# Build order of the adjacency tiles in a graph network kernel: halves of the four densest tiles placed between the others

## Chip, cores and metric

The kernel runs on one core of one Trainium2 chip. The metric is the device time of one execution in microseconds (us); below, the median of three executions and one execution with the hardware profiler.

## What is computed

The graph has 6250 nodes with 64 features and 200000 edges, sorted by destination. Destinations follow 6250 u² with u uniform, so low node numbers have many more edges than high ones. Two layers of mean aggregation (SAGE) come first, then three message-passing layers, each block with a residual and a layer norm:

```python
def sage_conv(x, src, dst, W_l, b_l, W_r, n_nodes):
    agg = segment_sum(x[src], dst, n_nodes)
    cnt = segment_sum(ones, dst, n_nodes)
    return agg / maximum(cnt, 1.0) @ W_l.T + b_l + x @ W_r.T

h = relu(sage_conv(x, ..., W_l1, b_l1, W_r1)); out = sage_conv(h, ..., W_l2, b_l2, W_r2)
x = layernorm(x + out)

def _mp_layer(x, src, dst, ea, W, b):      # self loops added
    m = concatenate([x[dst], x[src], ea], axis=1) @ W.T + b
    return relu(segment_sum(m, dst, n))
# three such layers, batch norm and relu after the first two
x = layernorm(x + _mp_layer(...))
```

Every aggregation is the same product: the matrix A of edge counts (source by destination) times node features. The kernel builds A once and uses it five times.

## The kernel before

**A in tiles.** Nodes are padded to NB = 49 blocks of 128. A is cut by destination into NT = 13 tiles of 512 columns (the last has 128, with 106 nodes). A tile `a` is [128, 49 x 512] in fp8: row p of block h is source 128 h + p. Its buffers come from the pool `fadj` with three buffers, which also holds, at the start, the edge list and the search table (`scratch`, L729).

**Windows and slots.** `window_plan` (L434) divides each tile's destinations into windows of w neighbouring nodes and gives each window k slots, a slot being 128 edges, from the expected number of edges alone. The plan has 2569 slots. By tile, 0 to 12: 655, 280, 256, 190, 171, 171, 171, 149, 128, 128, 128, 120 and 22. Dense tiles have narrow windows (one node at first, several slots each), later tiles wide ones (four nodes, one slot each). The windows of tile 0 average 92 columns (49 w) a slot, those of tile 8 have 196. Slots are numbered in build order and grouped by 128 into the columns t of a table. Where the edges of a window start is found by a search on the device (`near_samples`, `first_edges`, L787 to L820), in five groups of table columns; `SEARCH` (L417) says at which t each group's two steps are issued. `columns(t)` (L859) gathers the edges of 128 slots with one indirect DMA on GpSimd's queue and makes the keys: source low part, and source high part combined with the destination in the window.

**Build of a tile** (`build`, L896). For each slot, DVE makes two one-hot matrices by comparison with an iota (`one_hots`, L598): `lo` (128 columns, for 16 slots at a time, three buffers) and `rhs` (49 w columns, for a run of slots, three buffers). PE multiplies them into `pair` (L931), a PSUM tile of two banks, two buffers. When both banks are complete, ACT writes them to the fp8 tile (L938 for two equal banks at once, L943 one by one). After its last window the tile is stored to DRAM on SP's queue (L947). The last tile is first cleared by a memset on GpSimd (L903).

**First layer** (`first_layer`, L684). As soon as a tile is built, it is used from SBUF: `aggregate` (L618) issues 4 x 49 matmuls of 193 columns (L628: three bf16 parts of the features and a column of ones for the count) into one PSUM tile `agg` from a pool with one buffer. DVE reads it (L689, L653), counts are inverted (L690, L691, L695), and PE and ACT go on with a transpose (L678), a product (L698), a relu, a product (L703) and the split of the result into the bf16 parts of the second layer's input (L705 to L709).

**Order.** The loop at L1003 emits tile j's build and then the first layer of tile j - 1. A scheduler with its own cost model then fixes the order on each engine, so that matmuls of aggregation and build alternate on PE. [...] After the loop the slot buffers and PSUM banks are released (`slots.close()`), and the first layer of the last two tiles follows. `relative_dst` (L965), three DVE operations, and 72 small index loads on SP's queue (L959) prepare the edge attributes; they are emitted during the build.

**Second layer and the rest.** The second layer (L1032) starts with tiles 0 and 1 together, reloaded from DRAM (`load_adj`, L655): with `src_first` it goes over the 49 source blocks b and for each over the eight destination blocks, so that it can begin before the last blocks of the second layer's input exist. Beside it the edge attributes are summed (L976, L997). The three message layers (L1128) use A again.

Of the kernel before, what the change touches and what calls it, by code (L numbers as in the profile page):

```python
# [15 lines left out]
I32 = mybir.dt.int32  # L16
# [6 lines left out]
P = 128  # L23
TW = 512
# [427 lines left out]
    return tiles  # L452


@with_exitstack
def gnn_kernel(ctx: ExitStack, tc: tile.TileContext, x, src, dst, ea, W_l1, b_l1, W_r1, W_l2, b_l2, W_r2,
               W0, b0, W1, b1, W2, b2, g0, be0, g1, be1, out):
# [21 lines left out]
    def tw(j):  # L479
        return min(TW, NPAD - j * TW)  # L480

    wins = window_plan(N, E)
    slot_of, table = [], []
    for ws in wins:
        for d0, w, k in ws:
            slot_of.append(len(table))
            table += [(d0, s * P) for s in range(k)]
    NS = len(table)
    R = -(-NS // P)
# [1 line left out]
    for b in range(NB):  # L491
        n, c = slots_for(expected(N, E, b * P, (b + 1) * P)), 0
# [34 lines left out]
    adj8 = [dram.tile([P, NB * tw(j)], mybir.dt.uint8, name=f"adj8_{j}") for j in range(NT)]  # L527
    ok_t = None

    with ExitStack() as fast:  # L530
# [12 lines left out]
        apool = fast.enter_context(tc.tile_pool(name="fadj", bufs=3))  # L543
# [71 lines left out]
            w = tw(j)  # L615
            return a[:, : NB * w].rearrange("p (i w) -> p i w", w=w).bitcast(F8)

        def aggregate(psa, pt, tiles, n, src_first=False, feed=None, terms=None):  # L618

            views = [view(a, j) for a, j in tiles]
            sums = [psa.tile([P, 4, TW // 2], F32, name="agg") for _ in tiles]
            blocks = [(k, i) for k, (_, j) in enumerate(tiles) for i in range(tw(j) // P)]

            def product(k, i, b):

                nc.tensor.matmul(sums[k][:, i, :n], views[k][:, b, i * P: (i + 1) * P], pt[:, b, :n],  # L628
                                 start=(b == 0 and terms is None and not (src_first and i % 2)), stop=(b == NB - 1),
                                 skip_group_check=src_first or terms is not None)  # L630

            def term(k, i):
                if terms is not None:
                    at = tiles[k][1] * TW + i * P
                    nc.tensor.matmul(sums[k][:, i, : terms[1].shape[1]], terms[0][:, at: at + P], terms[1],  # L635
                                     start=not (src_first and i % 2), stop=False, skip_group_check=True)

            if src_first:
                for k, i in blocks:
                    term(k, i)  # L640
                for b in range(NB):
                    feed(b)
# [69 lines left out]
        with ExitStack() as bld:  # L712
# [180 lines left out]
                    made[c // HOT] = lo  # L893
                return made[c // HOT][:, c % HOT, :]

            def build(j):  # L896

                a = apool.tile([P, NB * TW], mybir.dt.uint8, name="a")
                av = view(a, j)
                ws = wins[j]  # L900
                done = sum(len(q) for q in wins[:j])
                if (j + 1) * TW > N:
                    nc.gpsimd.memset(a.bitcast(I32), 0)  # L903

                todo, banks, at = [], [], 0
                for q, (d0, w, k) in enumerate(ws):
# [4 lines left out]
                    todo += [(slot_of[done + q] + s, w * NB, len(banks) - 1, at, s == 0, s == k - 1) for s in range(k)]  # L911
                    at += w * NB

                runs = []
# [6 lines left out]
                pair = rhs = None  # L921
                for e, (slot, wc, bank, col, first, last) in enumerate(todo):
# [18 lines left out]
                    else:  # L941
                        for two, (o, nd) in enumerate(of):
                            nc.scalar.activation(av[:, :, o: o + nd],  # L943
                                                 pair[:, two, : nd * NB].rearrange("p (d h) -> p h d", h=NB),
                                                 AF.Copy, saturate=False)
                eng = nc.sync
                eng.dma_start(adj8[j], a[:, : NB * tw(j)])  # L947
                return a

            ids = room[:, 2 * size: 2 * size + 4 * NSUB * EAG].bitcast(I32).rearrange("p (i g) -> p i g", g=EAG)  # L950
# [48 lines left out]
                    if i == last_b[b]:  # L999
                        nc.scalar.activation(ext[:, b * P: (b + 1) * P], ps[:, :P], AF.Identity, bias=selfl)  # L1000

            prev = None
            for j in range(NT):  # L1003
                a = build(j)
                if j == 7:
                    relative_dst()
                if j == NT - 1:
                    break
                if prev is not None:
                    first_layer(psa1, prev, j - 1)  # L1010
# [188 lines left out]
```

## Time and profile before

| | |
|---|---|
| median of three executions | 1677.59 us (1675.6 to 1678.23) |
| profiled execution | 1678.72 us |
| its span, first to last instruction | 1676.9 us |
| granted TensorE clock, mean | 0.962 |
| busy PE, DVE, ACT | 1499.6, 923.4, 580.8 us |
| first build matmul starts | 43.36 us |
| stores of the built tiles 0 to 12 start (L947) | 167.1, 222.8, 261.9, 306.9, 344.3, 378.1, 411.8, 447.8, 482.7, 516.9, 551.2, 594.6, 608.9 us |
| aggregation (L628), whole kernel | 12005 matmuls, 1103.1 us busy |
| build matmuls (L931) | 2569 matmuls, 264.5 us busy |
| one-hots for the build on DVE (L598), lo and rhs | 194.8 and 236.0 us busy |
| evictions on ACT (L938) | 292.3 us busy |

Busy time is the union of an engine's instructions. The line of an operation made in a helper is that of the helper, so the one-hots of the build and of the edge attributes share L598. A matmul's end is modelled, so the busy time of PE also contains some waiting. "Waited" times name the instruction that came last. In a row of the stage table, the mark (x...) counts instructions.

### The profile page before, as it was taken

The numbers are of one execution on the slowest core, as the hardware profiler recorded it, in microseconds if no ns is written. First come the engines' busy times: TensorE is split into PE (matmuls) and PEld (weight loads), VectorE is DVE, ScalarE is ACT, GpSimd is POOL, SyncE is SP. The second block draws the span as 40 slices with busy tenths as digits, with TensorE's granted clock in tenths as the row PEclk, the third lists the DMA queues.
The fourth block names the chain that finished last, engine by engine and source line by source line (L and its number), as shares of the span: only waits on it lengthen the run. The fifth ranks groups of instructions, "written<-read, shape, count | busy, mean of one in ns | idle before, by whom it ended". The sixth has DMA issues, their size and how long they took to land.

```text
span 1676.9 us, 38592 instructions
## 1 busy us (share of the span) xinstructions
PE 1499.6 (89%) x17135; PEld 1383.0 (82%) x17135; DVE 923.4 (55%) x1581; ACT 580.8 (35%) x1085; POOL 82.3 (5%) x72
## 2 busy tenths in 40 slices
PE   1454989999999889999999999999999999999997
PEld 0343877788888779889999989988899999899997
DVE  2999999998788741988787721011241110342122
ACT  1233466787688640454454400000220000210000
POOL 2223100000000110000000000000000000000000
PEclk9965999999999989999999999999899999899999
DMA  5111232113211153635452634343416352345440
GB/s 161 30 29 50 97 93 83 80 81 152 86 78 78 79 205 159 259 138 182 144 204 75 248 143 166 154 169 130 184 58 251 155 218 110 155 166 231 165 183 10
DMA packets 43811, 228.10 MB, mean 136 GB/s; under 512 B 22978, under 2 KB 30210, under 8 KB 35826
## 3 DMA queue, kind: packets, MB, share of 16 engines
q1 hardware_dynamic: 37058, 139.54, 22.1%
q10 hardware_dynamic: 4496, 79.48, 12.1%
q0 software_dynamic: 2080, 6.52, 1.4%
q8 instruction: 136, 2.23, 0.5%
q14 instruction: 41, 0.34, 0.1%
HBM read 183.76 MB, written 41.75 MB: 134 GB/s over the span
## 4 chain that ended last, share of the span: by engine, by line
PE 62%; DVE 21%; ACT 7%; issue 5%; DMA 3%; ACTq 0%; POOL 0%; DVEq 0%; POOLq 0%
PE agg L628 47%; DVE lo L598 8%; PE pair L931 6%; ACT a L938 4%; DVE rhs L598 4%; PE u L1079 2%; PE bank L997 2%; DMA a<-adj 1%; PE agg L635 1%; DVE e L990 1%; DVE e L988 1%; DVE nd L653 1%; PE lin L1100 1%; PE lin L698 1%; PE tr L678 1%
## 5 line engine op out<-in xcount | busy, mean ns | idle before, releaser
L628 PE MATMUL agg<-parts,a 128*128 128x192 bf16 (+1 forms) x12005 | 1103.1, 248 | 7.6 <-DVE nd L653 4.8
L628 PEld LDWEIGHTS <-a 128*128 128x128 fp8e3 x12005 | 1012.5, 98 | 32.6 <-issue 17.4
L938 ACT ACTIVATE a<-pair 128x784 fp8e3<-128x784 f32 (+3 forms) x357 | 292.3, 886 | 120.8 <-PE pair L931 119.1
L931 PE MATMUL pair<-rhs,lo 128*128 128x147 bf16 (+5 forms) x2569 | 264.5, 243 | 73.6 <-DVE lo L598 50.2
L931 PEld LDWEIGHTS <-lo 128*128 128x128 bf16 x2569 | 195.9, 105 | 121.1 <-DVE lo L598 66.1
L598 DVE TENSOR_TENSOR rhs<-iota,k 128x1960 bf16<-128x1960 f16 (+14 forms) x240 | 236.0, 1006 | 12.8 <-ACT k L883 7.0
L598 DVE TENSOR_TENSOR lo<-iota,k 128x2048 bf16<-128x2048 f16 x161 | 194.8, 1220 | 0.0
L653 DVE TENSOR_REDUCE z<-agg 128x256 f32<-128x768 f32 (+1 forms) x39 | 35.3, 910 | 282.7 <-PE agg L628 282.4
L598 DVE TENSOR_TENSOR lo<-iota,e_d 128x2048 bf16<-128x2048 f16 (+11 forms) x132 | 130.9, 1012 | 20.6 <-PE bank L997 19.9
L997 PE MATMUL bank<-lo,lhs 128*128 128x128 bf16 x1701 | 107.6, 220 | 16.2 <-ACT lhs L991 10.8
L997 PEld LDWEIGHTS <-lhs 128*128 128x128 bf16 x1701 | 98.4, 98 | 27.4 <-ACT lhs L991 18.2
L653 DVE TENSOR_REDUCE nd<-agg 128x256 f32<-128x768 f32 (+1 forms) x26 | 23.5, 907 | 116.0 <-PE agg L628 116.0
L680 ACT COPY mx<-tr 128x512 f32<-128x512 f32 (+1 forms) x26 | 14.6, 560 | 177.5 <-PE tr L678 177.5
L1087 DVE BATCH_NORM_STATS2 stats<-hr 64x6 f32<-64x512 f32 (+1 forms) x26 | 17.0, 652 | 101.7 <-ACT hr L1102 80.4
L669 ACT ACTIVATE sp_r<-z 128x256 f32<-128x256 f32 (+1 forms) x26 | 10.5, 403 | 171.5 <-DVE z L668 171.4
L1116 ACT ACTIVATE hr<-tr 64x512 f32<-64x512 f32 (+1 forms) x13 | 7.4, 566 | 179.9 <-PE tr L1115 179.9
L987 ACT CAST lhs<-e 128x512 bf16<-128x512 f32 (+21 forms) x72 | 36.1, 502 | 58.9 <-PE bank L997 44.6
L991 ACT CAST lhs<-e 128x512 bf16<-128x512 f32 (+21 forms) x72 | 36.4, 505 | 23.0 <-DVE e L990 22.4
L988 DVE TENSOR_TENSOR e<-e,lhs 128x512 f32<-128x512 f32 (+21 forms) x72 | 39.5, 552 | 8.3 <-ACT lhs L987 8.2
L989 ACT CAST lhs<-e 128x512 bf16<-128x512 f32 (+21 forms) x72 | 36.3, 504 | 22.2 <-DVE e L988 21.1
L990 DVE TENSOR_TENSOR e<-e,lhs 128x512 f32<-128x512 f32 (+21 forms) x72 | 39.4, 548 | 7.3 <-ACT lhs L989 6.7
L864 POOL DMA_INDIRECT rows<-cmb_d,start_i x21 | 30.8, 1465 | 251.0 <-ACT key L875 207.4
(140 smaller groups left out, 784.8 us busy)
## 6 DMA issues: line engine op xcount, KB each, us to landing
a<-adj SPq DMA_DIRECT2D x24, 3136.0 KB, 11.8
a<-adj ACTq DMA_DIRECT2D x24, 3136.0 KB, 11.3
adj<-a SPq DMA_DIRECT2D x12, 3136.0 KB, 9.8
e<-in_edge_attr_dram SPq DMA_DIRECT2D x25, 256.0 KB, 2.6
a<-adj SPq DMA_DIRECT2D x4, 784.0 KB, 4.6
out_dram<-z SPq DMA_DIRECT2D x12, 128.0 KB, 14.3
a<-first_edges ACTq DMA_DIRECT2D x1, 1216.0 KB
e<-in_edge_attr_dram SPq DMA_DIRECT2D x7, 152.0 KB
```

Source lines behind the costliest of these rows:

```text
L598: nc.vector.tensor_tensor(to.rearrange("p g (h two) -> p g h two", two=2), iota[:, :n].rearrange("p (h two) -> p h two", two=2).unsqueeze( ...
L628: nc.tensor.matmul(sums[k][:, i, :n], views[k][:, b, i * P: (i + 1) * P], pt[:, b, :n], start=(b == 0 and terms is None and not (src_first ...
L653: nc.vector.tensor_reduce(to, ps[:, :nb, : 3 * D].rearrange("p b (r d) -> p b d r", r=3), AX.X, ALU.add)
L931: nc.tensor.matmul(pair[:, bank % 2, col: col + wc], lo_hot(t, c), rhs[:, i, :wc], start=first, stop=last)
L938: nc.scalar.activation(av[:, :, o: o + 2 * nd].rearrange("p h (two d) -> p h two d", two=2), pair[:, :, : nd * NB].rearrange("p two (d h) ...
L987: nc.scalar.copy(lhs[:, :g, 0:EC], r)
L988: nc.vector.tensor_sub(r, r, lhs[:, :g, 0:EC])
L989: nc.scalar.copy(lhs[:, :g, EC:2 * EC], r)
L990: nc.vector.tensor_sub(r, r, lhs[:, :g, EC:2 * EC])
L991: nc.scalar.copy(lhs[:, :g, 2 * EC:3 * EC], r)
L997: nc.tensor.matmul(ps[:, :P], lhs[:, q, :], oh[:, q % HOT, :], start=(c == 0 and q == 0), stop=(i == last_b[b] and q == g - 1))
L1079: nc.tensor.matmul(u[:, i, :], y[:, i * P: (i + 1) * P], maps[n - 1], start=True, stop=True)
```

## The change

A new function makes a list of units. Each of the four densest tiles (0 to 3) is divided into two halves of about equal cost; the halves stand between the other tiles. The list is 4, 0a, 5, 0b, 6, 1a, 7, 1b, 8, 2a, 9, 2b, 10, 3a, 11, 3b, 12, with slots 171, 330, 171, 325, 171, 139, 149, 141, 128, 128, 128, 128, 128, 106, 120, 84, 22. Slots are numbered in this order, so the table of the search and the gathers follow it. A half-built tile keeps its buffer until the second half is done; only then is it stored and given to the first layer. The second layer's first pair goes over the source blocks in the order in which the first layer was emitted. The first layer of a whole tile is emitted after the build of the following unit; after the last but one whole tile the two remaining ones (3 and 12) are done behind `slots.close()`. The three operations of `relative_dst` are emitted at unit 10 in place of tile 7.

```diff
+def build_order(wins, dense=4):
+    halves = []
+    for j in range(dense):
+        cost, half = 0, sum(k * (6 + w) for _, w, k in wins[j]) / 2
+        for q, (_, w, k) in enumerate(wins[j]):
+            cost += k * (6 + w)
+            if cost >= half:
+                break
+        halves += [(j, wins[j][: q + 1], False), (j, wins[j][q + 1:], True)]
+    order = []
+    for j in range(dense, len(wins)):
+        order.append((j, wins[j], True))
+        if halves:
+            order.append(halves.pop(0))
+    assert not halves
+    return order
...
-    for ws in wins:
+    order = build_order(wins)
+    table, first_slot = [], []
+    for _, ws, _ in order:
+        first_slot.append(len(table))
         for d0, w, k in ws:
-            slot_of.append(len(table))
             table += [(d0, s * P) for s in range(k)]
...
-                                 start=(b == 0 and terms is None and not (src_first and i % 2)), stop=(b == NB - 1),
+                                 start=(b == sources[0] and terms is None and not (src_first and i % 2)), stop=(b == sources[-1]),
...
-                for b in range(NB):
+                for b in sources:
                     feed(b)
...
-            def build(j):
-                a = apool.tile([P, NB * TW], mybir.dt.uint8, name="a")
+            built = {}
+            def build(u):
+                j, ws, last_step = order[u]
+                if j not in built:
+                    built[j] = apool.tile([P, NB * TW], mybir.dt.uint8, name="a")
+                    if (j + 1) * TW > N:
+                        nc.gpsimd.memset(built[j].bitcast(I32), 0)
+                a = built[j]
...
-                eng = nc.sync
-                eng.dma_start(adj8[j], a[:, : NB * tw(j)])
+                if not last_step:
+                    return None
+                nc.sync.dma_start(adj8[j], a[:, : NB * tw(j)])
                 return a
...
-            prev = None
-            for j in range(NT):
-                a = build(j)
-                if j == 7:
+            prev, ready = None, []
+            for u, (j, _, _) in enumerate(order):
+                a = build(u)
+                if u == 10:
                     relative_dst()
-                if j == NT - 1:
+                if u == len(order) - 1:
                     break
                 if prev is not None:
-                    first_layer(psa1, prev, j - 1)
-                prev = a
+                    first_layer(psa1, *prev)
+                    ready.append(prev[1])
+                prev = (a, j) if a is not None else None
...
-            first_layer(psa, prev, NT - 2)
-            first_layer(psa, a, NT - 1)
+            for a, j in (prev, (a, j)):
+                first_layer(psa, a, j)
+                ready.append(j)
...
-            pair = aggregate(psa, parts[1], [(load_adj(j), j) for j in range(2)], 3 * D, True, lambda b: None)
+            pair = aggregate(psa, parts[1], [(load_adj(j), j) for j in range(2)], 3 * D, True, lambda b: None,
+                             sources=[b for j in ready for b in range(j * TW // P, (j * TW + tw(j)) // P)])
```

More of the change, by code (lines that the diff above doesn't have):

```diff
@@ L482, in gnn_kernel @@
     wins = window_plan(N, E)
-    slot_of, table = [], []
-    for ws in wins:
+    order = build_order(wins)
+    table, first_slot = [], []
+    for _, ws, _ in order:
+        first_slot.append(len(table))
         for d0, w, k in ws:
-            slot_of.append(len(table))
             table += [(d0, s * P) for s in range(k)]
@@ L616, in view, with aggregate @@
             return a[:, : NB * w].rearrange("p (i w) -> p i w", w=w).bitcast(F8)
-        def aggregate(psa, pt, tiles, n, src_first=False, feed=None, terms=None):
+        def aggregate(psa, pt, tiles, n, src_first=False, feed=None, terms=None, sources=range(NB)):
             views = [view(a, j) for a, j in tiles]
@@ L894, in lo_hot @@
                 return made[c // HOT][:, c % HOT, :]
-            def build(j):
-                a = apool.tile([P, NB * TW], mybir.dt.uint8, name="a")
+            built = {}
[6 more added lines that the diff above has]
+                a = built[j]
                 av = view(a, j)
[L900 to L903, printed above, removed]
+                done = first_slot[u]
                 todo, banks, at = [], [], 0
-                for q, (d0, w, k) in enumerate(ws):
+                for d0, w, k in ws:
                     if not banks or banks[-1][1] + w > MAXW:
@@ L910, in build @@
                     banks[-1][1] += w
-                    todo += [(slot_of[done + q] + s, w * NB, len(banks) - 1, at, s == 0, s == k - 1) for s in range(k)]
+                    todo += [(done + s, w * NB, len(banks) - 1, at, s == 0, s == k - 1) for s in range(k)]
+                    done += k
                     at += w * NB
```

## Prediction

> **What bounds the kernel now.** I read the slices of the page first, then a table of busy time by stage, then the waits, then single pieces of the timeline. The slices say that only the front of the kernel can gain from another build order:
>
> ```profile
> PE   1454989999999889999999999999999999999997
> DVE  2999999998788741988787721011241110342122
> PEclk9965999999999989999999999999899999899999
> ```
>
> Each digit is a slice of 42 us. PE is at 4 or 5 tenths in slices 2 to 4 while DVE is full; from slice 6 on PE is full. Cutting the table at the stores of the built tiles (L947) gives one row per tile, 0 to 12. Columns are stretch, length, then PE, PEld, DVE, ACT and POOL busy, granted clock, DMA:
>
> ```profile
> 42.00:167.10 125.10, 62.52 (x745) 49.30 (x746) 118.69 (x225) 38.90 (x65) 34.23 (x23) 0.72 0.13 37
> 167.10:222.83 55.73, 47.38 (x487) 41.02 (x485) 55.40 (x75) 28.07 (x37) 5.86 (x5) 0.93 0.25 77
> 222.83:261.92 39.09, 36.26 (x479) 32.20 (x476) 37.17 (x52) 28.40 (x37) 2.77 (x2) 0.96 0.32 98
> 261.92:306.88 44.96, 42.11 (x400) 33.19 (x398) 44.96 (x61) 29.70 (x49) 3.25 (x2) 1.00 0.19 76
> 306.88:344.30 37.42, 35.74 (x382) 30.62 (x379) 36.83 (x50) 28.77 (x41) 2.60 (x1) 1.00 0.22 89
> 344.30:378.06 33.76, 32.26 (x369) 28.59 (x370) 30.60 (x42) 27.82 (x39) 2.44 (x2) 1.00 0.25 101
> 378.06:411.81 33.75, 31.98 (x369) 28.35 (x367) 32.04 (x47) 28.23 (x39) 3.44 (x2) 1.00 0.25 101
> 411.81:447.76 35.95, 34.82 (x383) 31.24 (x381) 27.97 (x44) 27.50 (x41) 0.94 (x1) 1.00 0.22 93
> 447.76:482.65 34.89, 33.86 (x351) 30.20 (x349) 26.84 (x34) 26.71 (x40) 0.00 (x0) 1.00 0.22 94
> 482.65:516.88 34.23, 33.20 (x343) 29.55 (x341) 26.84 (x34) 26.71 (x40) 0.00 (x0) 1.00 0.23 95
> 516.88:551.20 34.32, 33.17 (x342) 29.42 (x340) 26.68 (x33) 26.77 (x39) 0.00 (x0) 1.00 0.22 95
> 551.20:594.63 43.43, 37.06 (x336) 31.16 (x334) 32.96 (x40) 29.51 (x40) 6.28 (x2) 0.92 0.19 77
> 594.63:608.89 14.26, 7.15 (x44) 4.44 (x42) 6.50 (x17) 8.07 (x17) 0.59 (x2) 0.85 0.98 393
> ```
>
> Tiles 0 to 4 last as long as DVE is busy (302.3 us); tiles 5 to 10 as long as PE is (206.9 us) while DVE is busy 27 to 32 us of 34. Tile 0 has no aggregation beside it, so PE waits there for one-hots:
>
> ```profile
> PEld L931 <- DVE lo L598: 66.1, 69, 4.0
> PE pair L931 <- DVE lo L598: 50.2, 54, 3.8
> ```
>
> Tile 11 holds a stall. A GpSimd memset (L903) and a small DVE operation (L690) start on the end of one aggregation, and DVE's takes 4.48 us (mean of the group 0.52); the chain behind it leaves DVE idle another 7.2:
>
> ```profile
> 551.76 5.32 POOL L903 MEMSET a<- 128x6272 int32 x1 [128.15 <-PE agg L628]
> 552.63 4.48 DVE L690 TENSOR_SCALAR inv<-cnt 128x4 f32<-128x4 f32 x1
> ```
>
> **What the skill says.** (1) "TensorE: Matmul & The Clock Gate", Back-to-back issue gap: an isolated warm matmul costs N/2.4 + 2.5 ns. That is 82.5 ns for 192 columns; the trace's 304 aggregation matmuls in 25.24 us at 644.7 are 83. It warns that small N costs more; 16 build matmuls of 49 columns took 0.85 us at 43.4, 53 ns. (2) Same page, What's actually happening: the array drops to half clock when little used and returns on sustained use. Agrees: 0.72 in tile 0, 0.93 to 1.00 after. (3) "SBUF — State Buffer", SBUF: two separate sides: GpSimd and certain DVE modes exclude each other on a port pair. The 4.48 us fits.
>
> **The parts.** The window plan, slot count (2569), one-hot operations and first-layer sums are the same; listing both programs shows equal counts on PE and DVE.
>
> *PE prices.* Build: 84 ns per 196-column slot, so tile 8 costs 128 x 0.084 = 10.8 us. By columns (0.43 ns each, at least 53 ns a slot) tiles 5 to 11 cost 10.8 each, 4 12.9, 3 19.1, 2 13.6, 1 22.0, 0 34.7. Tiles 5 to 10 took 206.9 us; less 6 x 10.8 this leaves 23.7 us for one first-layer aggregation with its transposes and switches, 0.121 us per matmul of 196. It is the critical term; pure matmuls would be 16.2 and the fp32 steps beside them some 4.4, so 20.6 is its lower bound.
>
> *PE slack is what can be won.* Tiles 0 to 4 need on PE 34.7 + 22.0 + 13.6 + 19.1 + 12.9 + 4 x 23.7 = 197 of 302: 105 us slack.
>
> *New front: 4, 0a, 5, 0b.* Still bound by DVE, since only the aggregations of 4 and 5 exist to fill it. DVE of tiles 0, 4, 5 is 118.7 + 36.8 + 30.6 = 186.1; search steps of tables 5 and 6, which ran in tile 1, come here (4.7), as does one of the three relative-position operations (2.55); tile 0's idle stays (125.1 - 118.7 = 6.4). Sum 199.7. PE needs 34.7 + 12.9 + 11 + 2 x 23.7 = 106: slack 94. So only 11 of 105 us are recovered. The first dense tile is still built almost alone.
>
> *The other twelve units, 6 to 3b.* PE: builds 10.8 x 6 + 22.0 + 13.6 + 19.1 = 119.5, nine aggregations 213.3, sum 332.8. DVE, same tiles less what moved and less the memset's 4.4, is 299. PE bounds them, if it is never idle. In the changed program's order, aggregation of an ordinary tile already runs in the second half of its own build (106 matmuls in tile 7, 120 in 9 and 11), and the rest in the dense half after it. Unit by unit, the larger of PE and DVE is 34.3, 34.6, 30.5, 24.1; 32.9, 30.5, 26.8, 18.6; 32.9, 32.2, 28.6, 22.5: sum 348.5. The 15.7 between the sums is what DVE can or cannot save by running ahead. One-hot buffers hold two or three groups of 16 slots (some 6 us of DVE), enough for most of it at the three crossings from full to light units. I take 335.5.
>
> *Ends.* The memset still waits for the aggregation of the tile whose buffer it takes (now 10), as does L690 of that tile: tile 11's excess, 43.4 - 34.5 (mean of tiles 8 to 10) = 8.9, stays; 0 if it misses. Tile 12 stays 14.3: its chain of transposes and one-hots is the same. Its two deferred aggregations are now 3 and 12, with the same 245 matmuls. The source order of the second layer gains 0: it must end with the blocks of tiles 3 and 12, and its second adjacency load waits for the last full aggregation (628.55) whatever the order; bound 0 to 1 us either way.
>
> *Costs at nothing.* Splitting makes 39 in place of 34 single evictions and 355 in place of 357 merged ones: 3 x 0.6 = 2 us on ACT, which has over 6 us idle in most stages. Half-built tiles hold one of three buffers longer; tile 5's evictions wait for tile 4's aggregation and store. In program order the aggregation ends during 0a, 117 slots earlier, so nothing waits; without that cover it would be up to 24 us. On SP, two adjacency stores now precede the 36 index loads, and tile 0's store follows them (some 31 us on the queue in the profile); its buffer is wanted again only two units later. GpSimd's gathers keep their order.
>
> *Sum.* 42 before the first build + 199.7 + 335.5 + 8.9 + 14.3 = 600.4, against 608.9: 8.5 less. The remaining 1068.0 of the span is unchanged: 1668.4, with the 1.8 around it 1670.2. The profiled execution (1678.72) was 1.1 above the median, so I forecast 1669 as median.
>
> **Rivals.**
> A. Forecast, 4 to 16 us saved: chance 0.50, 1669.
> B. Aggregation gets cheaper between dense halves: 9 x 3.1 = 28 us less PE, then DVE's 299 to 305 bounds those units: saves 30 to 40, about 1641; anything beyond 16 saved counts here. For it: the pure rates. Against: six stages in a row cost 23.7. Chance 0.15.
> C. A wash, within 3.4 us: half of the 15.7 is lost, 540.5 + 65.2 = 606 for 608.9, about 1675. Chance 0.17.
> D. Slower. The units add up singly: DVE can't run ahead across a boundary, since its queue also waits for the aggregation's results in between. Place: the crossings after 1a, 2a and 3a. Price: 15.7, giving 42 + 199.7 + 348.5 + 23.2 = 613.4, 4.5 more: about 1682. It decides once less than 3 us of the 15.7 is recovered. For it: tiles 0 to 4 are bound by one engine and 5 to 10 by the other. Against: tile 4, with both near 36, took only 0.6 more than DVE. Chance 0.18, half-clock stretches in the halves of 0 included.
> That the order doesn't do what it says is excluded: the listed program interleaves the halves.
>
> **Numbers.** Faster by over 0.2% (3.4 us, about what a measurement of this kernel can tell from no change): A and B, 0.65. Same: 0.17. Slower: 0.18. The range runs from 1652 (a third to half of B) to 1684 (D with 2 us of ACT): it leaves out most of B and D's tail.
>
> **What would show it.** Right: tile 0's second half is stored near 242 us with DVE full up to there; PE full from there to some 577; the last build store near 600. Wrong: an aggregation stage well off 23.7 (B); DVE idle in 7, 9, 11 or PE idle in light units (D); clock under 0.8 in 0a or 0b; the memset off the chain.

## The result, and the profile after

The changed kernel takes 1657.25 us (median of four runs, 1655.67 to 1657.64) beside 1677.91 us for the kernel before (four runs, 1675.6 to 1679.2). The ratio is 0.9877, 95% interval 0.9859 to 0.9894: 20.7 us less where 8.5 were forecast. The direction held and the time lies inside the range; the size was missed by more than a factor of two.

Lines of the changed kernel are some 20 to 30 higher: one-hots L620, build matmuls L958, evictions L965 and L970, aggregation L650, the tile store L975, the gather of a table column L886, the memset L926, the small operation behind it L712. In the experiments' kernels the same lines stand within about 10 of these.

The profiled execution took 1656.98 us, span 1655.2. The same three rows of the page's slices:

```profile
PE   1586789899998989999999999999999999999997
DVE  2999999998898733897888610001340100442122
PEclk9697899999999999999999999999899999899999
```

The second to fourth slice of PE went from 4, 5 and 4 tenths to 5, 8 and 6, and the fifth from 9 to 7, with DVE full in all four. The stage table, cut at the stores, now has 13 rows, because a first half is not stored: 4; 0a+5; 0b; 6; 1a+7; 1b; 8; 2a+9; 2b; 10; 3a+11; 3b; 12. Columns as before: stretch, length, PE, PEld, DVE, ACT, POOL busy, clock, DMA:

```profile
42.00:89.66 47.66, 30.29 (x199) 21.67 (x199) 45.54 (x81) 34.41 (x61) 8.87 (x6) 0.64 0.09 25
89.66:186.04 96.38, 67.26 (x773) 54.69 (x774) 92.68 (x172) 39.14 (x54) 29.18 (x19) 0.81 0.20 71
186.04:231.78 45.74, 37.23 (x534) 33.19 (x533) 45.74 (x68) 20.77 (x26) 3.55 (x3) 0.91 0.28 87
231.78:266.39 34.61, 33.76 (x391) 30.01 (x389) 32.38 (x45) 29.09 (x40) 2.45 (x2) 1.00 0.36 111
266.39:330.11 63.72, 58.96 (x618) 50.57 (x616) 62.72 (x88) 43.08 (x68) 16.83 (x3) 1.00 0.13 54
330.11:353.25 23.14, 21.82 (x247) 19.26 (x245) 23.14 (x26) 14.22 (x18) 22.84 (x2) 1.00 0.34 143
353.25:383.10 29.85, 29.70 (x310) 26.72 (x308) 28.50 (x41) 26.25 (x41) 4.02 (x3) 1.00 0.29 116
383.10:441.17 58.07, 55.54 (x636) 49.66 (x634) 48.38 (x73) 42.23 (x64) 2.51 (x2) 1.00 0.14 59
441.17:456.58 15.41, 14.52 (x210) 12.66 (x208) 15.41 (x20) 12.34 (x14) 0.00 (x0) 1.00 0.50 211
456.58:483.55 26.97, 26.96 (x278) 24.06 (x277) 26.97 (x31) 25.49 (x39) 0.00 (x0) 1.00 0.29 121
483.55:553.26 69.71, 63.69 (x636) 54.84 (x634) 53.88 (x75) 45.55 (x69) 6.28 (x2) 0.98 0.12 48
553.26:571.76 18.50, 17.80 (x155) 13.94 (x154) 18.41 (x22) 13.27 (x21) 0.00 (x0) 1.00 0.49 194
571.76:586.40 14.64, 7.98 (x38) 5.34 (x38) 6.34 (x15) 8.02 (x16) 0.59 (x2) 0.77 0.93 362
```

The last build store starts at 586.40 instead of 608.89, 22.5 us earlier; the rest of the span is 1068.8 instead of 1068.0. So the whole gain lies before that store. About 1.2 us of it is the start: the first build matmul comes at 42.18 instead of 43.36, and in the experiments below it lies anywhere between 40.4 and 43.1 (e15 to e17 apart). Summed over the two tables, the build did the same work with fewer holes: DVE busy 500.1 (503.5 before), DVE idle 44.3 (63.4); PE busy 465.5 (467.5), PE not busy 78.9 (99.4). In the first three rows (the front) DVE is busy for all but 5.8 us, and PE has room. Behind it the rows differ. PE is the fuller engine in 6, 8, 2a+9 and 3a+11; DVE is in 1a+7 (62.7 of 63.7 us) and in the short rows 1b, 2b and 3b, where PE is nearly full too; in 10 both are full. The two waits of PE for low one-hots, over the whole run, have shrunk by a third and more:

```profile
PEld L958 <- DVE lo L620: 45.4, 64, 4.0
PE pair L958 <- DVE lo L620: 30.3, 31, 3.8
```

And the pair of GpSimd's memset and the small DVE operation is still there, now 33 us earlier:

```profile
518.22 5.33 POOL L926 MEMSET a<- 128x6272 int32 x1 [89.31 <-PE pair L958]
519.09 4.48 DVE L712 TENSOR_SCALAR inv<-cnt 128x4 f32<-128x4 f32 x1
```

### The profile page after: what moved, and what is told of

The parts are those of the page before. It is cut to its first block, busy times and chain, and to the rows that moved or that the text cites. A ratio compares the mean times of both kernels' runs of the same rounds, so it can differ in the third digit from the quotient of the medians.

```text
span 1655.2 us, 38577 instructions
## 1 busy us (share of the span) xinstructions
PE 1496.9 (90%) x17135; PEld 1379.9 (83%) x17135; DVE 920.0 (56%) x1581; ACT 578.4 (35%) x1088; POOL 117.0 (7%) x72
## 3 DMA queue, kind: packets, MB, share of 16 engines
q1 hardware_dynamic: 37058, 139.54, 22.4%
## 4 chain that ended last, share of the span: by engine, by line
PE 62%; DVE 21%; ACT 7%; issue 5%; DMA 3%; ACTq 0%; POOL 0%; DVEq 0%; POOLq 0%
PE agg L650 47%; DVE lo L620 7%; PE pair L958 6%; DVE rhs L620 4%; ACT a L965 4%; PE u L1110 2%; PE bank L1025 2%; DVE e L1016 1%; PE agg L657 1%; DVE e L1018 1%; DMA e<-in_edge_attr_dram 1%; DVE nd L675 1%; PE tr L700 1%; PE lin L1131 1%; DMA a<-adj 1%
## 5 line engine op out<-in xcount | busy, mean ns | idle before, releaser
L650 PE MATMUL agg<-parts,a 128*128 128x192 bf16 (+1 forms) x12005 | 1089.8, 246 | 5.6 <-DVE nd L675 1.8
L650 PEld LDWEIGHTS <-a 128*128 128x128 fp8e3 x12005 | 1008.3, 98 | 23.6 <-issue 12.1
L965 ACT ACTIVATE a<-pair 128x784 fp8e3<-128x784 f32 (+3 forms) x355 | 292.3, 890 | 122.8 <-PE pair L958 121.2
L958 PE MATMUL pair<-rhs,lo 128*128 128x147 bf16 (+5 forms) x2569 | 266.2, 244 | 64.0 <-DVE lo L620 30.3
L958 PEld LDWEIGHTS <-lo 128*128 128x128 bf16 x2569 | 196.2, 104 | 119.4 <-issue 52.1
L620 DVE TENSOR_TENSOR rhs<-iota,k 128x1960 bf16<-128x1960 f16 (+15 forms) x240 | 238.9, 1015 | 13.6 <-ACT k L905 11.3
L620 DVE TENSOR_TENSOR lo<-iota,k 128x2048 bf16<-128x2048 f16 x161 | 194.5, 1215 | 0.0
L620 DVE TENSOR_TENSOR lo<-iota,e_d 128x2048 bf16<-128x2048 f16 (+11 forms) x132 | 130.7, 1010 | 20.6 <-PE bank L1025 19.8
L886 POOL DMA_INDIRECT rows<-cmb_d,start_i x21 | 64.8, 3084 | 207.4 <-ACT key L897 167.0
L1118 DVE BATCH_NORM_STATS2 stats<-hr 64x6 f32<-64x512 f32 (+1 forms) x26 | 17.0, 653 | 101.7 <-ACT hr L1133 80.4
L702 ACT COPY mx<-tr 128x512 f32<-128x512 f32 (+1 forms) x26 | 14.6, 562 | 166.9 <-PE tr L700 166.8
L691 ACT ACTIVATE sp_r<-z 128x256 f32<-128x256 f32 (+1 forms) x26 | 10.5, 403 | 171.4 <-DVE z L690 171.4
L1126 POOL TENSOR_TENSOR nd<-res,inv 128x256 f32<-128x256 f32 (+1 forms) x13 | 7.6, 589 | 550.5 <-DVE ln_s L688 339.2
L1019 ACT CAST lhs<-e 128x512 bf16<-128x512 f32 (+21 forms) x72 | 36.4, 505 | 23.1 <-DVE e L1018 22.6
L1016 DVE TENSOR_TENSOR e<-e,lhs 128x512 f32<-128x512 f32 (+21 forms) x72 | 39.4, 550 | 8.9 <-ACT lhs L1015 8.8
## 6 DMA issues: line engine op xcount, KB each, us to landing
a<-adj SPq DMA_DIRECT2D x24, 3136.0 KB, 12.4
a<-adj ACTq DMA_DIRECT2D x24, 3136.0 KB, 11.5
```

The lines of the kernel that those rows point to most:

```text
L620: nc.vector.tensor_tensor(to.rearrange("p g (h two) -> p g h two", two=2), iota[:, :n].rearrange("p (h two) -> p h two", two=2).unsqueeze( ...
L886: pin(nc.gpsimd.indirect_dma_start(out=rows, out_offset=None, in_=cmb_d[:, :], in_offset=bass.IndirectOffsetOnAxis(ap=start_i[:, t: t + 1] ...
L958: nc.tensor.matmul(pair[:, bank % 2, col: col + wc], lo_hot(t, c), rhs[:, i, :wc], start=first, stop=last)
L965: nc.scalar.activation(av[:, :, o: o + 2 * nd].rearrange("p h (two d) -> p h two d", two=2), pair[:, :, : nd * NB].rearrange("p two (d h) ...
L1016: nc.vector.tensor_sub(r, r, lhs[:, :g, 0:EC])
L1019: nc.scalar.copy(lhs[:, :g, 2 * EC:3 * EC], r)
```

## The experiments

The theory to test: the build consists of a front that DVE bounds and a stretch that PE bounds; time is won exactly where one engine's spare time is filled from the other's work. The rivals: the gain is all in the front (from splitting tile 0 alone); the gain comes from something else in the new order (the second layer's source order, aggregations that got cheaper). A ratio is to runs of the kernel before on the same chip, whose medians were 1679.1 to 1680.9; the changed kernel would be 1658 to 1660 beside those.

**Which engine bounds where.** Four kernels add work of one kind at one place to the changed kernel. e9 and e10 make the low one-hots of one table column twice (eight operations), column 2 in the front, column 13 behind it; e11 and e12 issue the first matmul of every window of one tile twice, tile 5 in the front, tile 8 behind it. The edits are shown for e9 and e11; e10 has t == 13 and e12 u == 8:

```diff
+                    if t == 2:
+                        one_hots(lo, k2[:, 1, c // HOT * HOT: (c // HOT + 1) * HOT, :], iota)
...
+                    if u == 2 and first:
+                        nc.tensor.matmul(pair[:, bank % 2, col: col + wc], lo_hot(t, c), rhs[:, i, :wc], start=first, stop=True)
```

> The changed kernel with the eight low one-hots of table column 2 made twice: 8 x 1.2 = 9 to 10 us more on DVE inside unit 0a, in the front. Slack theory: DVE bounds the front, so all of it is paid: 9 to 10 us more than the changed kernel, 1666 to 1668. Rival (the front waits for PE or for chains between engines): 4 us or less more.

> The same for table column 13 (second half of tile 8 and first of 2a), behind the front. Slack theory: PE bounds this stretch and DVE has 4 us to spare in tile 8 and 10 in 2a, so 0 to 3 us more: 1657 to 1660. Rival (DVE can't run ahead, each unit pays the larger of its engines and DVE's waiting is a part of the chain): 6 to 10 us more.

> The changed kernel with each build matmul of tile 5 that opens a sum issued twice (the second overwrites the first): 171 x 0.064 = 11 us more on PE in the front. Slack theory: PE idles there, so 0 to 2 us more, 1657 to 1659. Rival (PE sets the front, at its half clock): 6 us or more.

> The same for tile 8: 128 x 0.084 = 11 us more on PE behind the front. Slack theory: PE is the bound there, so 8 to 11 us more, 1665 to 1668. Rival (DVE bounds this stretch too, after smoothing): 4 us or less more.

| kernel | added work | median | ratio [95%] | over the changed kernel (1679.13 x 0.9877 = 1658.5) |
|---|---|---|---|---|
| e9 | DVE, front | 1667.79 | 0.9933 [0.9916, 0.9949] | +9.3 |
| e10 | DVE, behind | 1658.95 | 0.9880 [0.9863, 0.9896] | +0.5 |
| e11 | PE, front | 1660.79 | 0.9886 [0.9870, 0.9903] | +2.3 |
| e12 | PE, behind | 1669.15 | 0.9940 [0.9924, 0.9957] | +10.7 |

The stage of 0a+5 in e9 and e11, to be held against the row above (96.38):

```profile
88.86:195.72 106.86, 68.69 (x773) 56.25 (x774) 102.21 (x180) 39.18 (x54) 29.51 (x20) 0.79 0.19 64
87.79:187.00 99.21, 77.29 (x946) 66.42 (x947) 93.29 (x172) 40.17 (x54) 30.30 (x20) 0.83 0.20 70
```

And the stages of 8 and 2a+9 in e10 and e12 (29.85 and 58.07 above):

```profile
352.46:387.13 34.67, 33.02 (x345) 29.52 (x343) 33.31 (x48) 26.58 (x41) 4.02 (x3) 1.00 0.25 100
387.13:442.07 54.94, 52.64 (x602) 46.64 (x600) 51.50 (x70) 42.14 (x63) 3.49 (x2) 1.00 0.15 62
352.38:384.69 32.31, 31.83 (x327) 28.03 (x325) 31.10 (x48) 27.79 (x41) 2.74 (x3) 1.00 0.27 107
384.69:451.76 67.07, 65.12 (x747) 59.16 (x745) 46.16 (x66) 42.10 (x64) 16.47 (x2) 1.00 0.13 51
```

In e9 the stage is 10.5 us longer with DVE 9.5 busier and PE hardly changed; in e12 PE is 11.7 busier over the two stages, and they are 11.5 longer. The same work put at the other place costs 0.5 and 2.3, which the intervals can't tell from nothing (e11 and e12 came out one to two microseconds above what was expected): in e10 DVE is 7.9 us busier over the two stages, and they are 1.7 longer. Shown, at these places: in 0a+5 DVE sets the time and PE has room, in 8 and 2a+9 the reverse. The stretch of 1a+7 and 1b, where DVE is full, was not tested so.

**One part of the order alone.** e1 splits only tile 0 (4, 0a, 5, 0b, 1, 2, 3, 6 to 12), e2 moves whole tiles without a split (4, 0, 5, 1, 6, 2, 7, 3, 8 to 12), e3 leaves tile 0 first and whole and splits 1, 2 and 3 (0, 4, 1a, 5, 1b, 6, 2a, 7, 2b, 8, 3a, 9, 3b, 10, 11, 12). In each the edit is the list of tiles (`build_order` takes a list here, and `relative_dst` is emitted at the unit that holds slot 1900, which is unit 10 in the changed order):

```diff
-    plan = [4, 0, 5, 0, 6, 1, 7, 1, 8, 2, 9, 2, 10, 3, 11, 3, 12]
+    plan = [4, 0, 5, 0, 1, 2, 3, 6, 7, 8, 9, 10, 11, 12]
```

> Order 4, 0a, 5, 0b, then 1, 2, 3 whole and 6 to 12: only tile 0 is divided. Slack theory (the time won is PE's waiting time, and it is found wherever DVE's work lies without aggregation beside it): the front ends at 232 us as in the changed kernel; 1, 2, 3 take DVE's 130 us (PE needs 126); 6 to 11 take 6 x 34.5 + 9; last build store at 593 for 587, so 1663 us, 6 more than the changed kernel. Rival (each pair of a dense half and an ordinary tile earns its share): three quarters of the divided tiles are gone, so 1667 to 1673 us. Rival (the second layer's source order earns it): 1657 us.

> Order 4, 0, 5, 1, 6, 2, 7, 3, 8 to 12, all tiles whole. Slack theory: tiles 4 and 0 are DVE-bound to some 204 us with one aggregation beside them; from there PE is full: 130.5 us of builds and ten aggregations of 23.7, 9 of memset stall and 15 for tile 12 end the build at 595, so 1666 us, 9 more than the changed kernel; dividing a tile has no worth of its own. Rival (halves are needed so that no unit is bound by one engine alone): 1672 us or more.

> Order 0 whole first, then 4, 1a, 5, 1b, 6, 2a, 7, 2b, 8, 3a, 9, 3b, 10, 11, 12: the front of the kernel before with the rest of the changed one. Slack theory: tile 0 alone to 167 us as before; after it PE is full: 146 us of builds, eleven aggregations of 23.7, 9 and 15 end the build at 598, so 1667 us: half of the gain. Rival (all of the gain is tile 0 no longer built alone): 1676 us. Rival (pairs of a dense half and an ordinary tile earn it): 1660 us or less.

Measured: e1 1701.01, ratio 1.0112 [1.0093, 1.0132]; e2 1675.5, 0.9969 [0.9955, 0.9983]; e3 1682.76, 1.0012 [1.0003, 1.0021]. All three missed the time expected of them, e1 by 38 us, on the other side of zero. In e1 the front was as good as in the changed kernel (ended at 231.57), but then tiles 1, 2 and 3 stand one after the other (the profiled execution of e1 is its fastest, 1695.18):

```profile
231.57:290.77 59.20, 49.03 (x501) 41.88 (x500) 53.63 (x77) 30.43 (x44) 1.98 (x2) 0.94 0.22 65
290.77:339.35 48.58, 39.79 (x471) 35.48 (x470) 41.93 (x55) 28.25 (x38) 4.03 (x2) 0.84 0.17 70
339.35:394.43 55.08, 45.14 (x407) 36.03 (x406) 44.28 (x61) 31.44 (x52) 4.63 (x4) 0.92 0.16 64
```

They took 162.9 us; DVE was busy for 139.8 and neither engine was full. VectorE's longest wait in these three stages says why:

```profile
DVE hi L889 <- DMA rows<-cmb_d,start_i: 20.1, 4, 9.4
```

`hi` is the first operation on a gathered table column. It stands in VectorE's queue ahead of one-hots, and the wait stops the engine: in the piece below, ScalarE had finished the keys of the column before at 295.95, but the next one-hots start at 304.39, behind `hi`. (e1's waits for keys, 14.2 us over the run, lie in the stages of tiles 7 to 9, where PE is full; the kernel before has 14.4 there.) In the timeline of e1 the gather is issued beside the store of a whole tile:

```profile
290.77 0.33 SPq L971 DMA_DIRECT2D adj<-a  x1
291.20 3.08 POOL L882 DMA_INDIRECT rows<-cmb_d,start_i  x1 [52.91 <-ACT key L893]
300.45 0.23 DVE L889 TENSOR_SCALAR hi<-rows 128x128 int32<-128x128 int32 x1 [6.65 <-DMA rows<-cmb_d,start_i]
```

The gather had waited for its buffer of rows ("<-ACT key"), which the previous column gave back late. e7 is e1 with a third such buffer (and, to make room, one-hot groups limited to 1984 columns: five groups of 2000 become 1950, their number stays 242):

```diff
-                rows = ew.tile([P, P], I32, name="rows")
+                rows = ew.tile([P, P], I32, name="rows", bufs=3)
```

> The order 4, 0a, 5, 0b, 1, 2, 3, 6 to 12 of e1_only0, with three buffers in place of two for the edges that a gather brings in (and one-hot runs of at most 1984 columns, to make room). Theory (e1_only0 lost its time in the stages of tiles 1, 2 and 3 to gathers that were issued too late, 20 us of DVE's waiting): the gathers go out a table column earlier, that waiting goes, and the kernel takes 1675 to 1683 us for 1701. Rival (these stages are slow because DVE's and PE's work does not overlap there, and the gather's wait only names what came last): no change, 1698 us or more.

e7: 1681.04, ratio 1.0011 [1.0003, 1.0020]: 20 us better than e1. In the profiles (14.6 us apart) the waits for rows in the three stages fall from 20.1 to 5.8 us, and the stages from 162.9 to 150.2. So late gathers were about half of the 38 us by which e1 missed. The rest lies in the same stages: DVE is busy there for 139.8 us in e7 as in e1, where 130 had been expected, and idle for 10. With most of the late gathers mended, splitting tile 0 alone is no gain: tiles 0 to 5 are done at 380.39 in e7, at 378.06 in the kernel before.

In e3 DVE is busy for 239.0 of the first 251.1 us of the build (0, 4, 1a with 5, 1b, to 293.13), while PE is not busy for 76.9 of them (78.3 in the first five stages of the kernel before). e2 gains 5.2 us. In its stage of tile 1, 60.2 us, DVE is busy for 53.4 and waits 5.4 for rows, and PE is busy for 51.1; its stage of tile 3 is PE's already (45.1 of 46.1). From 42 us to the last build store PE is not busy for 99.4 us before, 91.5 in e2, 95.0 in e7, 101.7 in e3, and 78.9 in the changed kernel: the times follow PE's unused time. None of the three orders gives more than 5 of the 20.7 us, so neither the split front alone nor the interleaved rest alone does it here. The rival "all in the front" is out.

**The second layer's source order.** e4 is the changed kernel with the sources in natural order.

```diff
-                             sources=[b for j in ready for b in range(j * TW // P, (j * TW + tw(j)) // P)])
+                             sources=range(NB))
```

> The changed kernel with the second layer's first pair in the natural order of source blocks, 0 to 48, so that it meets the late blocks of tile 3 in its first third. Slack theory: the build is the same to the last store; the pair waits at blocks 12 to 15 for a few us at most, so 1657 to 1662 us. Rival (a good part of the gain is the second layer starting earlier by the new source order): 1667 us or more.

e4: 1662.17, ratio 0.9891 [0.9859, 0.9924], not told from the changed kernel. Its last build store is at 588.4 and the rest of its span 1071.9, against 1068.8. Even these 3 us are within the scatter: with the new order of sources e11 has 1073.4. The order of sources is not where the 20 come from.

**The memset.** e5 is the changed kernel with the memset cut to the 49 x 128 bytes that the last tile has; e6 is the same cut in the kernel before.

```diff
-                        nc.gpsimd.memset(built[j].bitcast(I32), 0)
+                        nc.gpsimd.memset(built[j][:, : NB * tw(j)].bitcast(I32), 0)
```

> The changed kernel with the clearing memset of the last tile cut to the columns that this tile has: 1568 words a partition in place of 6272, so some 1.3 us on GpSimd in place of 5.3. Theory that the memset's hold on DVE is on the chain (in the profile after it holds one small DVE operation for 4.48 us and PE's transposes behind it): the last build store comes 4 to 9 us earlier, 1648 to 1653 us. Rival (the stall falls into slack, since the unit before was PE-bound): within 2 us of the changed kernel.

> The kernel before with the same smaller memset. If the memset's stall is worth the same in both orders, as the prediction took it, 4 to 9 us less than before: 1669 to 1674 us. Rival (it fell into slack there): no change.

e5: 1653.54, ratio 0.9843 [0.9826, 0.9859], the fastest kernel of the study by median, if at the very edge of what the intervals tell from the changed kernel. The memset takes 1.41 us, the small operation 0.56, and the stage of 3a+11 is 66.24 us in place of 69.71 (with the long memset it is 70.1 to 70.3 in e4, e9, e11 and e12). e6: 1678.75, ratio 0.9995 [0.9987, 1.0004], nothing. There the memset is short too, but the gather of the last table column, which stood behind it on GpSimd's queue, goes out two microseconds after a tile's store, and the wait for its landing takes the place of the stall:

```profile
550.37 0.32 SPq L947 DMA_DIRECT2D adj<-a  x1
550.93 1.41 POOL L903 MEMSET a<- 128x1568 int32 x1 [127.06 <-PE agg L628]
551.80 0.56 DVE L690 TENSOR_SCALAR inv<-cnt 128x4 f32<-128x4 f32 x1
552.49 0.95 POOL L864 DMA_INDIRECT rows<-cmb_d,start_i  x1 [0.15 <-DVE inv L690]
561.84 0.23 DVE L871 TENSOR_SCALAR hi<-rows 128x128 int32<-128x128 int32 x1 [8.81 <-DMA rows<-cmb_d,start_i]
```

The prediction put the stall of tile 11 on the memset and the chain behind it. The stall has two members, and the late gather was hidden behind the memset. In the changed order no store goes out near this gather (it landed after 3.4 us), and removing the first is a gain.

**Finer pieces.** If halves are good, are quarters of tile 0 better? e8 has the small memset and the order 4, 0, 5, 0, 6, 0, 7, 0, 8, 1, 9, 1, 10, 2, 2, 11, 3, 12, with as many parts of a tile as it stands there.

> Tile 0 in four quarters between tiles 4, 5, 6, 7 and 8, tile 1 in halves between 8, 9 and 10, tiles 2 and 3 behind, with the smaller memset: order 4, 0, 5, 0, 6, 0, 7, 0, 8, 1, 9, 1, 10, 2, 2, 11, 3, 12. Slack theory: the front up to the last quarter is bound by DVE to 289 us, with four aggregations beside it in place of two; after it PE needs 264 us; the last build store comes at 577 less the memset's stall, so 1640 to 1650 us. Rival (the changed kernel has already what there is to win, PE is full behind the front): 1655 us or more. Late gathers, as in e1_only0, would show as DVE waiting for them.

e8: 1669.82, ratio 0.9945 [0.9929, 0.9961], 16 us slower than e5 and 20 above what was expected. Its waits for rows are 13.3 us and for keys 12.4 (2.3 and 3.0 in e5). e13 gives it the third buffer of rows, e14 gives it to e5.

> The quarters order of e8 with one more buffer for gathered rows, so that a gather may be issued before the tile stored last has left its rows. Theory (e8's miss is late gathers and the keys behind them, 13.3 us of waits for rows and 12.4 for keys): some 15 to 20 us come back, 1650 to 1657 us, with waits for rows below 6 us. Rival (the extra starts of parts and the switching between tiles cost it): within 5 us of e8, 1665 to 1670 us.

> The changed order with the small memset of e5 and one more buffer for gathered rows. In e5 few waits for rows are left (the units of one tile stand apart, so rows come free early): theory says within 3 us of e5, 1650 to 1656 us. If late gathers still bind in the changed order, 1643 to 1649 us.

e13: 1667.86, 0.9924 [0.9906, 0.9942], 2 us less by the medians, which the intervals don't tell from nothing; the waits for rows are still 8.7, for keys 14.4. e14: 1667.23, 0.9924 [0.9907, 0.9940], 14 us *slower* than e5, though it has one buffer more. Single gathers in e14 stand on GpSimd's queue for a long time:

```profile
201.37 30.66 POOL L882 DMA_INDIRECT rows<-cmb_d,start_i  x1 [0.71 <-ACT key L893]
335.83 24.09 POOL L882 DMA_INDIRECT rows<-cmb_d,start_i  x1 [39.69 <-ACT key L893]
373.85 18.58 POOL L882 DMA_INDIRECT rows<-cmb_d,start_i  x1 [13.94 <-ACT key L893]
```

The usual value is 0.95 to 1.93. VectorE's waits for rows in e14's build are 12.4 us in two pieces of 6.2 (2.3 in e5), in the stages of 6 and 2a+9, which are 6.0 and 8.8 us longer than in e5. The second is for the gather of 18.58 us, which ended at 392.43. The first is for one of 1.00 us, issued at 237.12, 4.4 us after a tile's store: in e14's order its `hi` stands only 6.8 us behind it, in e5 45.1 us. The two longest gathers of e14 let nobody wait for their data. The changed kernel has such a gather too, 33.35 us at 318.34, and its data landed 34.9 us after the issue; the column is wanted only at 365.8, so it costs nothing there. Most of these gathers ended about a microsecond after a run of one-hots on VectorE had ended (one in e13, of 34.71 us, ended two microseconds before the run did). In the changed kernel:

```profile
318.34 33.35 POOL L886 DMA_INDIRECT rows<-cmb_d,start_i  x1 [26.75 <-ACT key L897]
...
349.66 1.21 DVE L620 TENSOR_TENSOR lo<-iota,k 128x2048 bf16<-128x2048 f16 x1
350.80 0.15 DVE L711 COPY cnt<-agg 128x4 f32<-128x4 f32 x1
350.87 0.94 DVE L675 TENSOR_REDUCE nd<-agg 128x256 f32<-128x768 f32 x1
```

e15 to e17 were to break the runs by reductions on VectorE whose result nobody reads. The edit is e15's and e17's; e16 has a short reduction, [P, 1, P], after every block:

```diff
+                    lows.append(c)
+                    if len(lows) % 4 == 0:
+                        nc.vector.tensor_reduce(brk, iota[:, :P].unsqueeze(1).to_broadcast([P, 8, P]), AX.X, ALU.add)
```

> The kernel of e14 with a reduction of 1024 iota numbers (about 1.1 us on VectorE, one input, its result read by nothing) after every fourth block of low one-hots, 13 in all. In e14 three gathers stood on GpSimd's queue for 18.6 to 30.7 us, each until VectorE's unbroken run of one-hots ended. Theory (a run of one-hots keeps GpSimd from starting the gather's work, and the reduction lets it in): no gather above 12 us, waits for rows below 7 us in place of 12.4, and of the 13.7 us by which e14 is behind e5 at least 5 come back after the 6 that the reductions cost in the front: 1655 to 1663 us. Rival (gathers are long for another reason, as the added buffer's own order on the queue): gathers still above 18 us, 1668 to 1675 us.

> As e15, but a reduction of 128 numbers, about 0.2 us, after every block of low one-hots, some 52 in all. If any instruction of another kind between two one-hots is enough to let a gather in, no gather lasts above 4 us and the time is 1655 to 1664 us. If the gap must be as long as the gather's own 0.95 us, the long gathers stay, and it is 1667 to 1675 us.

> The kernel of e13 (quarters, three buffers for rows) with the reductions of e15. Theory: its gathers of 34.7 and 18.0 us fall below 12 us, and 3 to 12 us come back net of 7 us of reductions in the front: 1656 to 1665 us. Rival (the quarters' miss is added starts and switching): 1668 to 1676 us.

e15: 1691.95, 1.0063 [1.0040, 1.0085]. e16: 1655.99, 0.9853 [0.9829, 0.9876]. e17: 1694.3, 1.0070 [1.0044, 1.0095]. e15 and e17 missed what was expected by 29 us and more; e16 came out as expected for the case that a short reduction lets the gathers in. But they are no clean test. There were 40 and 161 reductions in place of 13 and 52 (48.8 and 45.9 us of DVE), and since they depend on nothing, the scheduler put them in bunches ahead of the runs, in e15 partly ahead of the first build matmul, which came at 54.19: there a gather of 33.08 us still stands beside an unbroken run. In e16 no gather lasts over 2 us, the waits for rows are 3.0, and the kernel is 11 us faster than e14 although it has the reductions on top. So the third buffer is not slow in itself. But two gathers of e16, at 320.44 and 322.31, pass in 1.57 and 1.93 us beside a run of the same one-hots as the one that held a gather in the changed kernel:

```profile
320.44 1.57 POOL L883 DMA_INDIRECT rows<-cmb_d,start_i  x1 [18.36 <-ACT key L894]
322.31 1.93 POOL L883 DMA_INDIRECT rows<-cmb_d,start_i  x1 [0.30 <-issue]
```

What decides whether a gather gets in is open. Nor do long gathers and time go together over all kernels: the changed kernel and e5 are fast with one of 33 us, e8 is slow with none above 3.4. What the quarters lost their 16 us to is open as well; their waits for rows and keys are the largest difference in the profiles, but the third buffer, meant to take the first away, took away only 4.6.

## Why the prediction was right or wrong

*The bound, and where it changes sides*: right for the front and for 8 and 2a+9, as e9 to e12 show. Tile 0's second half was forecast to be stored near 242 with DVE full up to there; it was stored at 231.78, DVE 184.0 of 189.8 us busy. "PE full from there" did not hold in 1a+7 and 1b, where DVE was full.

*The front, 199.7 forecast, 189.8 measured*: this is the step that failed, and it is 9.9 of the 14.0 us by which the last build store came before the forecast 600.4. The mechanism was right and the term was mis-sized: DVE's work in the front, 193.35 in the prediction's sum, was 184.0. It was no scatter of one profile: in e1, e4, e5, e7, e10, e11, e12 and e14, which have the same front, it ends between 230.2 and 233.0. By groups of operations, the stages of 0, 4 and 5 before and the front after:

| us of DVE | before | after |
|---|---|---|
| one-hots | 141.8 | 138.7 |
| search | 23.5 | 27.8 |
| splits | 14.9 | 14.7 |
| keys | 9.1 | 7.5 |
| first layer | 4.0 | 4.1 |
| relative positions | 2.5 | 2.5 |
| overlap of neighbours, taken off | 9.7 | 11.3 |
| busy | 186.1 | 184.0 |

The search came as forecast (+4.3 for 4.7). The relative-position operation was counted twice: one already lay in tile 4's stage, so 2.55 fell out. The rest is that a stage cut at a store is not the work of a tile: 3.1 us of one-hots and 1.6 of keys (seven table columns against six) lay in those three stages and not in the new front. Some 1.1 us of the one-hots is the first group, which the changed kernel finished at 42.12, so before the mark from which both are counted; the other 3.6 us were made ahead for the tiles behind. The tiles need the same one-hots in both kernels, so the forecast charged the front with work that it doesn't do. That this work costs nothing where it falls in the changed order was not tested by itself. Overlap (1.6) and the small terms make up the 9.35 by which DVE was below 193.35; idle time was 5.8 for 6.4.

*PE's price, 23.7 us for an aggregation*: right, and with it rival B is out. PE was busy for 322.8 us in the twelve units; less 119.5 of builds that is 22.6 for each of nine. By the same count, of busy time, tiles 5 to 10 before give 22.4. e5, where the memset is out of the way, spent 336.6 us there, at most 24.1 for each.

*The twelve units, 335.5 for a pooled sum of 332.8*: right in size, and in part by luck. They took 336.6 in e5 (e5 is the place to read it, as the stall was a separate term). Of the 15.7 us between pooled and unit-by-unit sums, 11.9 were saved, 13.0 forecast. Rival D, which took them for lost, is out. But the parts don't follow the picture of a PE that is never idle. In the changed kernel 6 to 1b took 121.5 us for 114.7 of pooled PE work, with DVE busy for 118.2: here DVE was nearer to being the bound. 8 to 2b took 103.3 for 106.3, and 10 to 3b, less the memset's 3.5, 111.7 for 111.8. The first excess and the second gain partly cancel. That DVE could run ahead because each dense half is followed by a lighter unit is the prediction's reading; no run varies the buffers of one-hots.

*The memset, 8.9*: mis-sized, the second part of the miss. In the changed kernel it costs 3.5 us of the stage of 3a+11 (69.71 to 66.24), not the 8.9 read off as tile 11's excess. e6 shows why the excess was no price of the memset: without it tile 11's stage still took 43.2 us, now with the wait for the late gather.

*"Only 11 of 105 us PE slack"*: wrong in both numbers. PE was not busy for 78.3 us in the first five stages before, and for 55.0 in the front after, so 23 were recovered. The 27 us between 105 and 78.3 lie in tile 0's stage: its build matmuls, priced at 34.7 us, kept PE busy for 54.7 (32 of 98 columns at 83.59 took 3.04, so 95 ns each, at a granted clock of 0.72 in this stage), and 8.0 went to work that is neither build nor aggregation.

*Ends and zero costs*: tile 12 14.64 for 14.3, the rest 1068.8 for 1068.0, the source order not told from zero. ACT's evictions, costed at nothing, hold PE for 19.9 us where they held it for 4.2, but 12.7 of these lie in the first two stages, where PE has room.

Three readings of lines were off without bearing on the result: the clock was 0.92 and 0.85 in tiles 11 and 12, so not 0.93 or more everywhere behind tile 0; L690's mean is 0.49 us; and the fp32 steps beside an aggregation, put at 4.4, keep PE busy for 3.2 in each of the stages of tiles 8 to 10.

In all: front -9.9, units and memset -4.4, tile 12 +0.3, which is 586.4 for 600.4.

## What to carry to other kernels

When two engines bound a loop in turn, price the phases by the work in them, counted by operations, and not by the stretch between two stores: an engine that runs ahead moves its work across the mark. A pooled sum over alternating pieces came out here, where one engine's excess over the other was about 5 us at each of three crossings and the buffers hold some 6; check it piece by piece, as errors can cancel, and see that no small wait (a gather) stands in the queue ahead of the filler work, as it did in e1. Before a stall is put on one cause, look what would arrive next: here taking away the memset won 3.5 us in one order and nothing in the other.

## What the runs showed of the hardware

A gather that goes out just before or beside the store of a whole tile (3136 KB, itself 9.6 us to landing) was late in these runs: in e6, issued 2.1 us after a store, it had 9.4 us between its start and its first use, 8.8 of them a wait. In the changed kernel, from 42 us on, the two gathers issued 0.3 and 1.3 us before a store landed after 8.7 and 7.7 us; without the long one below, the others with a recorded landing took 2.4 to 5.0. The store is named by its place in time alone; no run moved it by itself.

A gather issued on GpSimd's queue while VectorE goes through an unbroken run of one-hots (two inputs, both in SBUF) can take 15 to 35 us instead of 1 to 2. In the changed kernel it happened to one of 21; those at 130.58 and 158.64, also beside one-hots alone, took 1.9. The Trainium skill, "SBUF — State Buffer", SBUF: two separate sides, has a trap that looks like this: the descriptors of a DMA issued by GpSimd are written by GpSimd's cores, which certain VectorE operations lock out of a shared port. The same page's section Who interferes with whom says that `tensor_tensor` has no mode of that kind but contends with GpSimd's reads, and infers that descriptor writing is free of it. The traces here show a hold of 33 us beside a run of TENSOR_TENSOR alone. That doesn't decide about the inference: the gather also takes its offsets from a tile in SBUF (`start_i`), so the contention with reads would fit as well, and that the port is the cause at all was not isolated.
